# Two attention layers with mixture-of-experts and integer feed-forward: order of queues and small additions around the TensorE stream

## The chip, the cores and the metric

The kernel runs on one core of a Trainium2 chip, as one program. The metric is the device time in microseconds (us), of which a median of several runs is given. The engines are named as in the profile: PE is TensorE, PEld its weight loads, DVE is VectorE, ACT is ScalarE, POOL is GpSimd, SP is SyncE, which issues most of the transfers.

## What is computed

Eight sequences (B = 8) of 512 tokens with 512 features, in fp32, go through two post-norm layers:

```python
x = layernorm(x + L0_attn(x, ...))   # 16 heads of 32, causal softmax, biases on Q, K, V and the output
x = layernorm(x + L0_ffn(x, ...))    # 8 experts, top 2 of a softmax; LoRA on gate, gate/up and down
x = layernorm(x + L1_attn(x, ...))   # RMS-scaled input, 8 heads of 64, 2 key/value heads, no mask
x = layernorm(x + L1_ffn(x, ...))    # (wq - 128) * scale for gate, up, down; 1408 hidden, silu(gate) * up
```

In layer 0's attention, `scores = where(causal, -inf, q k^T / sqrt(32))`, then softmax and a product with v. In the experts, each token's two routing weights are divided by their sum, and the LoRA terms (`2 * B A`) may be added to the weights beforehand.

## The kernel before

**Layer 0's attention** (`attention0`, L1296) goes batch by batch, about 85 us each. A batch has four head groups g of four heads, and a group three units u of its keys (UNITS: key tile 0; tiles 1 and 3; tile 2). For each unit PE computes scores `sc` (`scores`, L1461), ACT takes their exponential into `p` (L1476), POOL clears the upper triangle of the diagonal blocks by an `affine_select` for each key tile of the unit (L1486), and later PE multiplies `p` by the values into `av` (L1503, `product`). DVE adds the units' `p` to a total (L1511), PE sums it into `rs` (L1518), and `normalise` (L1514) takes the inverse and scales `av` into `aoT` (L1522). `guard.watch_inverses` (L1076) adds the inverses to a running sum `g_total` on POOL; it is part of a check whether the fast path may be kept. The bias of the output projection is added to the residual `x` on POOL, all four tiles of a batch in one 128x2048 operation at group 2 (L1595).

Beside a batch's units, a list `todo[g, u]` (`plan`, L1527) puts other work of earlier batches: the output projection and layernorm of the batch before, its turn to features by rows (x1T), router logits (`score`, L1433), `choose` (top two, ranks), `dispatch`, and `one_hot` with `enter` (L1458, `Router.enter` L596), which writes a table of tokens through the PSUM bank `ps_table`. For most batches the turn goes through DRAM (class `Turn`, L83): DVE transposes 32x32 blocks, `out` (L100) writes them in four transfers (turned<-x1T), and `back` (L105) returns them as x1T in one transfer of 1 MB. LoRA terms of the experts are made beside u = 2's scores (`Experts.pair`, L805): ACT scales them, and for half of the weights a `load` brings the weights (merged<-in_gate_up), POOL adds the scaled term (L823) and a store writes them (L824); `merging` holds these for later units: load at unit n + i, add at n + 1 + i, store at n + 2 + i, for i = 0, 1. Next inputs are loaded by `load_xT` at g == 2 and `load_x` at g == 3, 1 MB each.

PE's order within a batch is written out; the order on DVE, ACT, POOL and SP in this stage is set when the kernel is built, by a scheduler with estimated times. The last batch's rest and the first tiles of the experts are interleaved at the end of `attention0`, with all engines in the written order: `tiles.step()` (L1013) does one tile of 128 tokens of one expert (gate and up `half`, turn of the hidden rows, `down`).

**The experts' stage** goes on with such steps. Rows of results are written to DRAM and gathered.

**Layer 1's attention** (`Attention1.run`, L1758) has DVE, ACT, POOL and PE in written order. A batch gathers two expert rows a token (`fetch`), adds them (`add`), sums them with the residual, turns the rows through DRAM (`Turn`), and computes its units. In `usual_pass` (L1953) the residual rows of batches 2 to 7 are loaded by SP at the start of this stage, twelve transfers of 512 KB, and after them the first integer weights and `w_out`.

**The integer FFN** (`IntegerFfn.run`, L1191) computes gate and up (ps_g, ps_u, L1222) and the output (ps_f, L1238), with x and h split in a high and a low part. Its first batch starts behind the last batch's residual and norm in layer 1 (`norm`, L1819, x L1804). Its last tile is normalised by `last_rows` (L1278): statistics on DVE, rstd on POOL, one `tensor_scalar` (L1288), and a store by ACT.

Of the kernel before, what the change touches and what calls it, by code (L numbers as in the profile page):

```python
# [19 lines left out]
NB = 8  # L20
# [62 lines left out]
class Turn:  # L83
# [21 lines left out]
    def back(self, room):  # L105
        self.nc.sync.dma_start(out=room, in_=self.dram.rearrange("p k i f -> p (k i f)"))
# [320 lines left out]
class Router:  # L427
# [4 lines left out]
    def __init__(self, env, keep, pool, small, tmp, dram):  # L432
# [39 lines left out]
        lane = pool.tile([P, 1], F32, name="r_lane")  # L472
# [4 lines left out]
        i = tmp.tile([P, S], F32, tag="r_inv", name="r_columns_i", bufs=2)[:, : E * E_TILES].bitcast(I32)  # L477
# [118 lines left out]
    def enter(self, ps, b, token, column, held, columns):  # L596
# [5 lines left out]
        nc.vector.tensor_tensor(self.table, ps, self.table, ALU.add)  # L602
        nc.vector.tensor_tensor(self.table, held, self.table, ALU.add)

# [4 lines left out]
    def soon(self, pool, ps, held):  # L609


        nc, half = self.nc, E // 2
        nc.tensor.matmul(ps, lhsT=self.ones, rhs=self.carry, start=True, stop=True)
        nc.vector.tensor_reduce(held, ps[:, :half], AX.X, ALU.min)
        nc.vector.tensor_scalar(held, held, float(SOON * P), None, ALU.is_ge)
        tokens = pool.tile([P, half, SOON], I32, name="t_soon")
        nc.vector.tensor_copy(tokens, self.by_expert()[:, :half, :SOON])
        return lambda e, j: tokens[:, e, j : j + 1]
# [10 lines left out]
    def tables(self, pool, ps, held):  # L629
# [9 lines left out]
        nc.vector.memset(tokens, 0)  # L639
        nc.tensor.matmul(ps, lhsT=self.ones, rhs=self.carry, start=True, stop=True)  # L640
        n_i = pool.tile([P, E], I32, name="t_n_i")
# [185 lines left out]
class Tiles:  # L827
# [185 lines left out]
    def step(self):  # L1013
# [10 lines left out]
        while self.fetched <= i + 10 and (self.fetched < self.n_soon or self.of_fixed is not None):  # L1024
            self.fetch(self.fetched)
            self.fetched += 1
        if i:
            self.down(i)
# [70 lines left out]
class IntegerWeights:  # L1099
# [16 lines left out]
    def load(self, pool, n, last):  # L1116
        start, end, unit = next(r for r in self.ranges if self.at < r[1] or r is self.ranges[-1])
        n = min(n, last - self.at, end - self.at)
        if n > 0:
# [3 lines left out]
            self.env.nc.sync.dma_start(out=slot, in_=src.rearrange("u p f -> p u f"))  # L1123
            self.slots.append((slot, self.at, n))
            self.at += n

# [18 lines left out]
class IntegerFfn:  # L1145
# [45 lines left out]
    def run(self, held_out, last_norm):  # L1191
        tc, nc, weights = self.env.tc, self.nc, self.weights
        with ExitStack() as phase:
            self.work = phase.enter_context(tc.tile_pool(name="d_work", bufs=1))
            self.p_gu = phase.enter_context(tc.tile_pool(name="d_gu", bufs=2, space=PSUM, reuse_waits="tile"))
            self.p_o = phase.enter_context(tc.tile_pool(name="d_o", bufs=1, space=PSUM, reuse_waits="tile"))
# [81 lines left out]
    def last_rows(self, b, t, x):  # L1278
# [8 lines left out]
        if t == NT - 1:  # L1287
            nc.vector.tensor_scalar(x, x, mv[:, 0:1], rstd, ALU.subtract, ALU.mult)  # L1288
# [4 lines left out]
        nc.scalar.dma_start(out=env.ins.out[b][ts(t, P), :], in_=x)  # L1293


def attention0(env, guard, keep, routes, experts, dram, p_mm, tiles_ctx):  # L1296
# [8 lines left out]
    with ExitStack() as phase:  # L1305
# [103 lines left out]
        turns = Turn(env, dram, NT, "turned0")  # L1409

# [3 lines left out]
        def blocks(b):  # L1414
# [5 lines left out]
            turns.back(flat)  # L1420
# [37 lines left out]
        def enter(rows, mm=mm, columns=HD):  # L1458
            router.enter(mm([P, E * E_TILES], "ps_table"), *rows, columns)

        def scores(b, g, u):  # L1461
# [22 lines left out]
            for kt in UNITS[u]:  # L1484
                first = p[:, :, at : at + P]
                nc.gpsimd.affine_select(out=first, in_=first, pattern=[[0, 4], [1, P]], compare_op=ALU.is_ge, fill=0.0,  # L1486
                                        base=0, channel_multiplier=-1)
                at += S - P * kt
            for thunk in merging.pop(n, []):
                thunk()  # L1490
# [23 lines left out]
        def normalise(b, g, acc):  # L1514
# [7 lines left out]
            nc.vector.tensor_tensor(aoTs[b][:, g, :], av, r_inv, ALU.mult)  # L1522
            guard.watch_inverses(r_inv)

        merging = {}

        def plan(b):  # L1527
# [26 lines left out]
            if b > 1:  # L1554
                todo[0, 0].append(lambda: choose(b - 2, mm=aside))
                todo[1, 0].append(lambda: dispatch(b - 2))
                todo[1, 2].append(lambda: enter(one_hot(b - 2, range(NT))))
# [21 lines left out]
        def soon():  # L1579
            tiles.of_soon = router.soon(routes, mm([P, E], "ps_count"), guard.routed[:, 0:1])  # L1580
# [7 lines left out]
        for b in range(NB):  # L1588
            todo, late = plan(b)
            for g in range(ND):  # L1590
                if g == 2:
                    if b + 1 < NB:
                        load_xT(b + 1)

                    nc.gpsimd.tensor_tensor(xs[b], xs[b], row[:, 1:2, :].to_broadcast([P, NT, D]), ALU.add)  # L1595
                if g == 3 and b + 1 < NB:
                    load_x(b + 1)
# [44 lines left out]
        choose(b, P)  # L1642
# [662 lines left out]
```

## Time and profile before

| | |
|---|---|
| median of 3 runs | 2105.66 us (2105.58 to 2105.78) |
| the profiled execution | 2106.08 us |
| its span | 2104.2 us |
| granted TensorE clock | 0.999 |
| PE busy | 2074.4 us |
| first matmul starts, last ends | 4.6 and 2095.25 us after the span's start |
| transfers issued by SP and ACT (queues q1, q10) | 175.34 and 1.07 MB |
| transfers issued by POOL (q0) | 34.61 MB |

Times of single events are counted from the span's start. Layer 0's attention takes the time to about 683 us, the experts to 1064, layer 1's attention to 1607 and the FFN to the end. "x <- y" in a line of waits means: an instruction of the first engine and line stood until the second was done; the numbers are us in all, times, and the longest.

### The profile page before, as it was taken

The numbers are of one execution on the slowest core, as the hardware profiler recorded it, in microseconds if no ns is written. First come the engines' busy times: TensorE is split into PE (matmuls) and PEld (weight loads), VectorE is DVE, ScalarE is ACT, GpSimd is POOL, SyncE is SP. The second block draws the span as 40 slices with busy tenths as digits, with TensorE's granted clock in tenths as the row PEclk, the third lists the DMA queues.
The fourth block names the chain that finished last, engine by engine and source line by source line (L and its number), as shares of the span: only waits on it lengthen the run. The fifth ranks groups of instructions, "written<-read, shape, count | busy, mean of one in ns | idle before, by whom it ended". The sixth has DMA issues, their size and how long they took to land. (4 is left out here: it accounts for less than half of the span.)

```text
span 2104.2 us, 35813 instructions
## 1 busy us (share of the span) xinstructions
PE 2074.4 (99%) x15074; PEld 1048.8 (50%) x15074; DVE 1270.6 (60%) x1963; ACT 606.8 (29%) x840; POOL 496.0 (24%) x488
## 2 busy tenths in 40 slices
PE   8999999999999999999999999999999999999998
PEld 2333333333334677774433333333335888888886
DVE  2666776776768623234257898887867644555443
ACT  2333433324333111111143333333332322222222
POOL 2343534434333221222042221223101000000000
PEclk9999999999999999999999999999999999999999
DMA  9020303415222568877451322132102311111000
GB/s 326 22 65 38 101 22 110 136 52 156 85 98 102 172 199 239 251 227 209 149 206 51 100 81 71 56 95 81 41 1 71 100 41 61 60 61 60 21 21 22
DMA packets 181946, 213.39 MB, mean 101 GB/s; under 512 B 72570, under 2 KB 125818, under 8 KB 178706
## 3 DMA queue, kind: packets, MB, share of 16 engines
q1 hardware_dynamic: 170496, 175.34, 26.8%
q0 software_dynamic: 10560, 34.61, 5.6%
q8 instruction: 121, 1.98, 0.4%
q10 hardware_dynamic: 722, 1.07, 0.1%
q14 instruction: 47, 0.39, 0.1%
HBM read 132.58 MB, written 78.40 MB: 100 GB/s over the span
## 5 line engine op out<-in xcount | busy, mean ns | idle before, releaser
L1077 POOL TENSOR_TENSOR g_total<-g_total,r_inv 128x512 f32<-128x512 f32 x64 | 90.1, 1408 | 488.3 <-DVE r_inv L1862 269.9
L1476 ACT ACTIVATE p<-sc 128x2048 f32<-128x2048 f32 (+1 forms) x96 | 153.0, 1594 | 174.7 <-PE sc L65 150.7
L1511 DVE TENSOR_TENSOR p<-p 128x1536 f32<-128x1536 f32 (+2 forms) x96 | 149.5, 1557 | 77.6 <-POOL p L1486 74.4
L1227 DVE SCALAR_TENSOR_TENSOR hT<-ps_u,vec,sg 128x512 f32<-128x512 f32 x88 | 65.6, 745 | 187.2 <-PE ps_u L1222 187.1
L1238 PE MATMUL ps_f<-ffn_w,h_half 128*128 128x512 f32 x664 | 168.1, 393 | 2.6 <-DVE h_half L1233 2.0
L958 PE MATMUL ps_gu<-xrT,experts 128*128 128x256 f32 x736 | 166.7, 380 | 0.4 <-DMA xrT<-pair 0.4
L958 PEld LDWEIGHTS ps_gu<-xrT,experts 128*128 128x128 f32 x736 | 139.5, 190 | 35.6 <-issue 19.2
L1832 ACT ACTIVATE p<-sc 128x1024 f32<-128x1024 f32 x128 | 124.2, 1022 | 100.2 <-PE sc L65 91.5
L1862 DVE RECIPROCAL r_inv<-r_inv 128x512 f32<-128x512 f32 x32 | 107.1, 3346 | 67.8 <-ACT r_inv L1074 67.8
L1238 PEld LDWEIGHTS ps_f<-ffn_w,h_half 128*128 128x128 f32 x664 | 122.9, 188 | 34.6 <-DVE h_half L1233 8.0
L1222 PE MATMUL ps_g<-x_high,ffn_w 128*128 128x512 f32 x352 | 137.3, 390 | 0.9 <-DVE x L1804 0.9
L1222 PE MATMUL ps_g<-x_low,ffn_w 128*128 128x512 f32 x352 | 137.2, 390 | 0.0
L1222 PE MATMUL ps_u<-x_low,ffn_w 128*128 128x512 f32 x352 | 137.1, 390 | 0.0
L1222 PE MATMUL ps_u<-x_high,ffn_w 128*128 128x512 f32 x352 | 137.1, 389 | 0.0
L65 PE MATMUL sc<-qT,kT 64*64 64x512 f32 x1024 | 124.7, 602 | 1.2 <-ACT qT L1729 0.9
L65 PE MATMUL ps_q<-experts 128*32 128x512 f32 x1024 | 120.8, 601 | 4.9 <-DMA experts<-in_xT 4.6
L65 PE MATMUL ps_v<-experts 128*32 128x512 f32 x1024 | 120.9, 595 | 0.0
L1851 PE MATMUL av<-p,v 128*64 128x512 f32 x512 | 120.9, 594 | 0.0
L1486 POOL TENSOR_SCALAR_AFFINE_SELECT p<-p 128x512 f32<-128x512 f32 x128 | 82.7, 657 | 157.6 <-ACT p L1476 155.0
L1225 ACT ACTIVATE sg<-ps_g,vec 128x512 f32<-128x512 f32 x88 | 60.6, 689 | 199.8 <-PE ps_g L1222 199.8
L65 PE MATMUL ps_o<-attn_out,aoT 128*64 128x512 f32 x512 | 116.4, 598 | 0.0
L65 PE MATMUL ps_k<-experts 128*32 128x512 f32 x1024 | 116.3, 595 | 0.0
(278 smaller groups left out, 3248.3 us busy)
## 6 DMA issues: line engine op xcount, KB each, us to landing
results<-y SPq DMA_DIRECT2D x68, 256.0 KB, 3.2
pair<-xrT SPq DMA_DIRECT2D x30, 512.0 KB, 3.0
xrT<-pair SPq DMA_DIRECT2D x120, 128.0 KB, 3.8
turned<-turned SPq DMA_DIRECT2D x56, 256.0 KB, 4.0
x<-in_x SPq DMA_DIRECT2D x8, 1024.0 KB, 8.6
rows<-x SPq DMA_DIRECT2D x32, 256.0 KB, 2.3
x<-rows SPq DMA_DIRECT2D x16, 512.0 KB, 12.5
experts<-in_xT SPq DMA_DIRECT2D x7, 1024.0 KB, 8.5
```

The costliest lines, as they stand in the source:

```text
L65: nc.tensor.matmul(out[m], lhsT=lhsT[:, m], rhs=rhs, start=start, stop=stop)
L958: nc.tensor.matmul(ps[:, j, :], lhsT=w, rhs=xT[:, c, :], start=c == 0, stop=c == ND - 1)
L1077: self.nc.gpsimd.tensor_tensor(self.total, self.total, r_inv, ALU.add)
L1222: nc.tensor.matmul(ps, lhsT=w[:, ts(dc, P)], rhs=x[:, dc, :], start=(dc, i) == (0, 0), stop=(dc, i) == (ND - 1, 1))
L1227: nc.vector.scalar_tensor_tensor(hT, u, vec[:, V_SU + c : V_SU + c + 1], sg, ALU.mult, ALU.mult)
L1238: self.nc.tensor.matmul(os[t], lhsT=h[:, ts(t, P)], rhs=self.weights(2 * NHID + c), start=(c, i) == (0, 0), stop=(c, i) == (NHID - 1, 1))
L1476: nc.scalar.activation(p, sc[:, :, :width], AF.Exp, scale=scale)
L1486: nc.gpsimd.affine_select(out=first, in_=first, pattern=[[0, 4], [1, P]], compare_op=ALU.is_ge, fill=0.0, base=0, channel_multiplier=-1)
L1511: nc.vector.tensor_tensor(total[:, :, P * kt :], total[:, :, P * kt :], p[:, :, at : at + w], ALU.add)
L1832: nc.scalar.activation(p, sc, AF.Exp, scale=scale)
L1851: nc.tensor.matmul(st["av"][HD * j : HD * (j + 1), :], lhsT=st["v"][:, kt, HD * j : HD * (j + 1)], rhs=p[:, j, :], start=kt == 0, stop=kt ...
L1862: nc.vector.reciprocal(r_inv, r_inv)
```

## The change

The edits, in the order of the diff:

- `Turn.back` hands out its instruction. In layer 0's attention `behind_return` makes `load_xT` (now at g == 0 from the second batch on), `load_x` and the merging transfers issue behind the last return in SP's queue.
- POOL's bias add goes tile by tile, 128x512 behind the selects of each group's unit 1 (the first batch keeps one add); the sum of inverses goes behind the select of the next unit 2.
- The table's bank is read ahead of the last normalisation in the last batch (`behind`). The count of `soon` is made in `tables`, from a kept copy of `carry`; `choose` of the last batch goes into the middle of a step (`amid`).
- Layer 1: the rows of batches 3 to 7 are loaded behind a batch's return by SP; the rows of batch 2, `w_out` and the first integer weights are issued by ScalarE in the first batch. The first batch's add of tile 0 of the next batch comes one step later.
- FFN: the pool of ps_o is opened before that of ps_g and ps_u, and two of layer 1's output banks use the other half of their tile; this maps the tiles to other banks. The last tile is normalised and stored in two halves, by SP and ScalarE.
- A constant of lane numbers shares a temporary tile (left out below).

```diff
     def back(self, room):
-        self.nc.sync.dma_start(out=room, in_=self.dram.rearrange("p k i f -> p (k i f)"))
+        return self.nc.sync.dma_start(out=room, in_=self.dram.rearrange("p k i f -> p (k i f)"))
...
-        nc.vector.tensor_tensor(self.table, ps, self.table, ALU.add)
+        read = nc.vector.tensor_tensor(self.table, ps, self.table, ALU.add)
...
+        return read
...
-    def soon(self, pool, ps, held):
+    def soon(self, pool):
...
-        nc.tensor.matmul(ps, lhsT=self.ones, rhs=self.carry, start=True, stop=True)
-        nc.vector.tensor_reduce(held, ps[:, :half], AX.X, ALU.min)
-        nc.vector.tensor_scalar(held, held, float(SOON * P), None, ALU.is_ge)
+        self.soon_carry = pool.tile([P, half], F32, name="r_soon_carry")
+        nc.vector.tensor_copy(self.soon_carry, self.carry[:, :half])
...
-    def tables(self, pool, ps, held):
+    def tables(self, pool, ps, held_soon, held):
...
+        half = E // 2
+        ps, soon = ps[:, :E], ps[:, E:]
...
+        nc.tensor.matmul(soon, lhsT=self.ones, rhs=self.soon_carry, start=True, stop=True)
+        nc.vector.tensor_reduce(held_soon, soon, AX.X, ALU.min)
+        nc.vector.tensor_scalar(held_soon, held_soon, float(SOON * P), None, ALU.is_ge)
...
             self.turn_rows(i, self.nc.scalar.copy)
...
-    def step(self):
+    def step(self, amid=lambda: None):
...
             self.fetched += 1
+        amid()
         if i:
             self.down(i)
...
 
-    def load(self, pool, n, last):
+    def load(self, pool, n, last, queue=None):
...
-            self.env.nc.sync.dma_start(out=slot, in_=src.rearrange("u p f -> p u f"))
...
+            if queue is not None:
+                return lambda: queue.dma_start(out=slot, in_=src.rearrange("u p f -> p u f"))
+            self.env.nc.sync.dma_start(out=slot, in_=src.rearrange("u p f -> p u f"))
...
+            self.p_o = phase.enter_context(tc.tile_pool(name="d_o", bufs=1, space=PSUM, reuse_waits="tile"))
...
-            self.p_o = phase.enter_context(tc.tile_pool(name="d_o", bufs=1, space=PSUM, reuse_waits="tile"))
...
         if t == NT - 1:
-            nc.vector.tensor_scalar(x, x, mv[:, 0:1], rstd, ALU.subtract, ALU.mult)
+            for i, queue in enumerate((nc.sync, nc.scalar)):
+                half = x[:, ts(i, D // 2)]
+                nc.vector.tensor_scalar(half, half, mv[:, 0:1], rstd, ALU.subtract, ALU.mult)
+                queue.dma_start(out=env.ins.out[b][ts(t, P), ts(i, D // 2)], in_=half)
...
-        nc.scalar.dma_start(out=env.ins.out[b][ts(t, P), :], in_=x)
+            nc.scalar.dma_start(out=env.ins.out[b][ts(t, P), :], in_=x)
...
         turns = Turn(env, dram, NT, "turned0")
+        returned = [None]
+
+        def behind_return():
+            return tc.issue_after(returned[0].ins) if returned[0] else ExitStack()
...
             turns.out(flat)
-            turns.back(flat)
+            returned[0] = turns.back(flat)
...
         def enter(rows, mm=mm, columns=HD):
-            router.enter(mm([P, E * E_TILES], "ps_table"), *rows, columns)
+            return router.enter(mm([P, E * E_TILES], "ps_table"), *rows, columns)
...
                 first = p[:, :, at : at + P]
-                nc.gpsimd.affine_select(out=first, in_=first, pattern=[[0, 4], [1, P]], compare_op=ALU.is_ge, fill=0.0,
-                                        base=0, channel_multiplier=-1)
+                select = nc.gpsimd.affine_select(out=first, in_=first, pattern=[[0, 4], [1, P]], compare_op=ALU.is_ge,
+                                                 fill=0.0, base=0, channel_multiplier=-1)
                 at += S - P * kt
-            for thunk in merging.pop(n, []):
-                thunk()
+            if u == 2 and inverses:
+                with tc.issue_after(select.ins):
+                    guard.watch_inverses(inverses.pop())
+            if u == 1 and b:
+                with tc.issue_after(select.ins):
+                    for t in ((0, 1), (2,), (3,), ())[g] if b == NB - 1 else (g,):
+                        x = xs[b][:, t, :]
+                        nc.gpsimd.tensor_tensor(x, x, row[:, 1, :], ALU.add)
+            elif (g, u) == (2, 1):
+                with tc.issue_after(select.ins):
+                    nc.gpsimd.tensor_tensor(xs[b], xs[b], row[:, 1:2, :].to_broadcast([P, NT, D]), ALU.add)
+            with behind_return():
+                for thunk in merging.pop(n, []):
+                    thunk()
...
             nc.vector.reciprocal(r_inv, r_inv)
-            nc.vector.tensor_tensor(aoTs[b][:, g, :], av, r_inv, ALU.mult)
-            guard.watch_inverses(r_inv)
-
-        merging = {}
+            normed[0] = nc.vector.tensor_tensor(aoTs[b][:, g, :], av, r_inv, ALU.mult)
+            if (b, g) == (NB - 1, ND - 1):
+                guard.watch_inverses(r_inv)
+            else:
+                inverses.append(r_inv)
+
+        merging, inverses, normed = {}, [], [None]
+
+        def behind(first, second):
+            tc.add_manual_dep(second.ins, first.ins.name,
+                              mybir.DependencyInfo(mybir.DependencyClass.NoSync, mybir.DependencyReason.DATA),
+                              reason="reads of a bank that is wanted")
...
-                todo[1, 2].append(lambda: enter(one_hot(b - 2, range(NT))))
+                if last:
+                    todo[1, 2].append(lambda: behind(enter(one_hot(b - 2, range(NT))), normed[0]))
+                else:
+                    todo[1, 2].append(lambda: enter(one_hot(b - 2, range(NT))))
...
         def soon():
-            tiles.of_soon = router.soon(routes, mm([P, E], "ps_count"), guard.routed[:, 0:1])
+            tiles.of_soon = router.soon(routes)
...
             for g in range(ND):
-                if g == 2:
-                    if b + 1 < NB:
+                if g == (0 if b else 2) and b + 1 < NB:
+                    with behind_return():
                         load_xT(b + 1)
-
-                    nc.gpsimd.tensor_tensor(xs[b], xs[b], row[:, 1:2, :].to_broadcast([P, NT, D]), ALU.add)
                 if g == 3 and b + 1 < NB:
-                    load_x(b + 1)
+                    with behind_return():
+                        load_x(b + 1)
...
         score(b)
-        choose(b, P)
+        tiles.step(lambda: choose(b, P))
...
-    return router, tiles, router.tables(routes, p_mm.tile([P, E], F32, tag="mm", name="ps_count"), guard.routed[:, 1:2])
+    return router, tiles, router.tables(routes, p_mm.tile([P, E + E // 2], F32, tag="mm", name="ps_count"), *(guard.routed[:, i : i + 1] for i in range(2)))
...
                 st["hT"] = own.tile([P, ND, S], F32, tag="hT", name="hT1")
-                self.turn.back(st["hT"].rearrange("p k s -> p (k s)"))
+                back = self.turn.back(st["hT"].rearrange("p k s -> p (k s)"))
+                if 2 <= b < NB - 1:
+                    with self.env.tc.issue_after(back.ins):
+                        self.load_rows(b + 1)
...
         state[0]["aoT"] = work.tile([P, ND, S], F32, tag="aoT", name="aoT1", bufs=2)
-        weights.load(work, 2, weights.FIRST)
+        load_first = weights.load(work, 2, weights.FIRST, nc.scalar)
...
-        for j in range(2):
-            nc.sync.dma_start(out=w_out[HD * j : HD * (j + 1), :, :],
-                              in_=env.ins.w_attn1[6 + 2 * j : 8 + 2 * j].rearrange("u (h p) f -> p (u h) f", p=HD))
+
+        def load_out():
+            for j in range(2):
+                nc.scalar.dma_start(out=w_out[HD * j : HD * (j + 1), :, :],
+                                    in_=env.ins.w_attn1[6 + 2 * j : 8 + 2 * j].rearrange("u (h p) f -> p (u h) f", p=HD))
+
...
                 todo[0] += [lambda t=t: pieces[1]["fetch"](t) for t in range(NT)]
+                todo[2] += [lambda: self.load_rows(2, nc.scalar), load_out]
+                todo[3].append(load_first)
...
                         todo[i + 2].append(lambda t=t: then["stat"](t))
-                for t, i in ((0, 1), (1, 2)) if first else ((0, 0), (1, 1), (2, 1), (3, 2)):
+                for t, i in ((0, 2), (1, 2)) if first else ((0, 0), (1, 1), (2, 1), (3, 2)):
...
         prepare_table(AF.Silu)
-        banks += [p_sc.tile([P, 2, S], F32, tag="sc", name="ps_o1")[:, 0, :] for _ in range(2)]
+        banks += [p_sc.tile([P, 2, S], F32, tag="sc", name="ps_o1")[:, 1, :] for _ in range(2)]
...
-                def load_rows(b):
+                def load_rows(b, queue=nc.sync):
...
-                        nc.sync.dma_start(out=env.xs[b][:, t : t + GAP // P, :], in_=rows.rearrange("(t p) d -> p t d", p=P))
+                        queue.dma_start(out=env.xs[b][:, t : t + GAP // P, :], in_=rows.rearrange("(t p) d -> p t d", p=P))
...
-            for b in range(2, NB):
-                load_rows(b)
+            attention.load_rows = load_rows
```

More of the change, by code (lines that the diff above doesn't have):

```diff
@@ L471, in __init__ @@
         nc.gpsimd.iota(i, pattern=[[0, 1]], base=0, channel_multiplier=1)
-        lane = pool.tile([P, 1], F32, name="r_lane")
+        room = tmp.tile([P, S], F32, tag="r_inv", name="r_columns_i", bufs=2)
+        lane = room[:, E * E_TILES : E * E_TILES + 1]
         nc.vector.tensor_copy(lane, i)
@@ L476, in __init__ @@
             nc.vector.tensor_scalar(self.signed[:, t : t + 1], lane, float(P * t - GAP + (P * t >= GAP)), None, ALU.add)
-        i = tmp.tile([P, S], F32, tag="r_inv", name="r_columns_i", bufs=2)[:, : E * E_TILES].bitcast(I32)
+        i = room[:, : E * E_TILES].bitcast(I32)
         nc.gpsimd.iota(i, pattern=[[1, E * E_TILES]], base=0, channel_multiplier=0)
```

## The prediction

> **What bounds the kernel now.** I read the page's busy times first.
>
> ```profile
> span 2104.2 us, 35813 instructions
> PE 2074.4 (99%) x15074; PEld 1048.8 (50%) x15074; DVE 1270.6 (60%) x1963; ACT 606.8 (29%) x840; POOL 496.0 (24%) x488
> ```
>
> TensorE (PE) is busy for 2074.4 of 2104.2 us at a granted clock of 0.999, and the change leaves its matmuls as they are: by the built orders of both kernels, one 128x8 count moves and a few groups swap places. So all that can be won is PE's idle time, 29.8 us: 4.6 before the first matmul, 9.0 after the last (2095.25 to 2104.25), 16.2 between. The chain of waits agrees: after PE no engine has over 4%.
>
> ```profile
> PE 42%; DVE 4%; POOL 1%; issue 1%; DMA 0%; ACT 0%; POOLq 0%; DVEq 0%; ACTq 0%
> ```
>
> Then PE's waits by what ended them (us in all, times, longest):
>
> ```profile
> PE ps_q L65 <- DMA experts<-in_xT: 4.6, 1, 4.6
> PE ps_f L1238 <- DVE h_half L1233: 2.0, 7, 0.5
> PE av L1503 <- POOL p L1486: 1.9, 3, 1.0
> PE ps_logits L504 <- DMA x1T<-turned: 1.8, 2, 1.5
> PE ps_x1T L1427 <- DVE g_routed L614: 1.5, 1, 1.5
> PE sc L65 <- ACT p L1476: 1.2, 1, 1.2
> ...
> PE ps_g L1222 <- DVE x L1804: 0.9, 1, 0.9
> ...
> PE ps_r L65 <- ACT logits L1440: 0.8, 1, 0.8
> PE ps_rank L65 <- DVE earlier L553: 0.7, 1, 0.7
> PE ps_f L1238 <- issue: 0.6, 1, 0.6
> ...
> PE rs L1859 <- DVE total L1840: 0.2, 1, 0.2
> ```
>
> About nine of these us belong to waits that the diff aims at. The timeline gives each a further cost: two matmuls in a row overlap, and a wait breaks that. A wait of 0.62 moved the next start by 0.78, one of 0.22 by 0.38; I add 0.165 to each.
>
> **Returns.** PE waits for the turned rows at 162.6 (0.30) and 417.5 (1.46): with the overlap 0.46 + 1.62 = 2.1. At 417.5 the timeline shows the cause: the writes of turned rows are issued at 400.1 to 403.9, the 1 MB load of x at 404.07, then the return at 408.74, which lands at 417.39, 8.6 us later. In the FFN stage a return with nothing ahead of it took 5.1 us (1935.77 to 1940.84). In the new order of SP's queue it stands ahead of x, so it should land at about 413.8; PE wants it at 416.06. Taken: 2.1 (0 to 2.1).
>
> **POOL.** At 163.9, 503.4 and 588.9 PE waits for the selects of unit u = 1: 0.27, 0.60, 1.01, with the overlap 2.4. The row ahead of them is the bias add, one 128x2048 of 4.55 us (498.21 to 502.73 in the second case). Four 128x512 adds cost about the 1.41 of the g_total row each, 5.6 for 4.55 a batch, but each stands behind u = 1's selects, and POOL, 24% busy, hides it. The g_total add (1.5) goes behind u = 2's select. A unit of PE's work is about 7 us; POOL's fullest now holds a select, g_total and two merged adds: 0.63 + 1.5 + 1.3 + 2.3 = 5.7. Taken: 2.4 (1 to 2.4); uncovered, POOL's extra 1.1 us a batch would cost up to 6 in six batches.
>
> **What the new SP order gives back.** Where the return is, one merged store and load now queue behind it, x's load follows, and then a load that waits for the store to land. In POOL's new order the merged add of the first load stands between u = 0's select and u = 1's two selects, in the three batches that merge through DRAM at that point (turned writes near 400, 486 and 571). Price: return 408.74 + 5.1 = 413.8; a store and a load of 256 KB behind it (two such stores landed 0.65 and 0.67 after a return at 586.08) bring the load to 415.2; the add takes 1.27 and the selects 1.23, so p is ready at 417.75, where av could start at 416.06 + 0.86 = 416.92. The wait is 0.8. The same sum gives 502.2 against 502.61 in the next batch and 587.65 against 587.67 in the third: nothing. Taken: -0.8 (0 to -3, if each landing is a microsecond late). The bias of x comes 20 us later, and xT is wanted a batch later: no cost.
>
> **Last batch and start of the experts.** The table bank was read late, so ps_x1T waits 1.46 at 649.1 and ps_q 0.35 after it. The read moves ahead of the last normalisation, but VectorE works without a pause from 634 to 653, and x1T still passes through it: I take 0.75 of the 1.8 + 0.33 (0 to 1.5). At 723.6 ps_r's wait of 0.76 + 0.165 goes, because a gate/up half is put before it; ps_rank, which waited 0.72 for VectorE 7 us later, now has VectorE's copy of y and two transposes (0.67 each) in its chain, and I add 0.5 to it. The wait of 0.44 + 0.165 for xrT at 758.4 probably goes, since a count and the tables stand ahead. Net +0.7 (-0.5 to 1.1). The select at 667 (1.19) and the wait at 670.7 (0.57) are not touched.
>
> **Layer 1's start.** Twelve loads, 6 MB, leave the front of SP's queue; the rest of rows and w_out is issued by ScalarE. The gathers of expert rows landed 7.9 us after issue in that crowd and about 4 later: with the first add moved one step, rs<-total (0.24 + 0.165) and two waits of 0.125 go: 0.6 (0.4 to 0.9). Before shows no such issues on ScalarE; SP's issues of the same tiles take 0.38 to 0.67, so four of them, 2.2 us, lie between two exps (end 1080.7 and start 1082.3). If that delay went through to rs at 1093.5 it would cost 1.6. Here the Trainium skill speaks against the change: "DMA: Bandwidth & Descriptors", section "Issuing engines are not separate DMA queues", says that loads from another issuer use the same 16 engines and save only issue time. By that rule ScalarE's queue gains nothing here, and may lose 1.6; by the rows the gain comes from 5 MB being asked for later, which it doesn't forbid. I keep 0.6 (-1.6 to 0.9).
>
> **FFN's start.** ps_g waits for x (0.85 + 0.165) behind VectorE's two parts; the new order of banks lets ps_f's halves interleave. hT's low half then waits for the x that POOL's rstd holds and a 1.22 conversion: ready at 1616.1, wanted at 1614.65, so a wait of 1.45 takes the place of 0.62 + 0.165 and of the split 0.33. Net 0.5 (0 to 1).
>
> **Last store.** The last 128x512 is normalised in 0.55 and its store takes 2.5 (2099.40 to 2101.91). In two halves on two queues, half a normalisation, about 0.25, and some transfer would be saved, less a second fixed cost. [...]by its rule on issuers the halves share the engines and it is nil. I take 0.2 (-0.1 to 0.5).
>
> **Sum.** 2.1 + 2.4 - 0.8 + 0.75 + 0.7 + 0.6 + 0.5 + 0.2 = 6.45. From the profiled execution (2106.08; 1.9 of it around the span of 2104.2) that is 2099.63; the median of the runs is 0.42 below it, so 2099.2.
>
> **Rivals.** (1) All targeted waits go and nothing returns: the upper ends, 2.1 + 2.4 + 1.5 + 1.1 + 0.9 + 1.0 + 0.5 = 9.5, give 2096.2. For it: 4 us of PE's work stand behind most waits. Against it: VectorE's unbroken stretch at 634 to 653. Chance 0.13.
>
> (2) The waits change their names: VectorE bounds 649, ps_rank and ps_f's low half as well as before, only the returns and half of the selects are won, less 0.8: 2.1 + 1.2 - 0.8 = 2.5, 2103.2. The case that the return, in the queue's real order, lands no earlier gives 2101.3. For it: VectorE is 60% busy, and turned writes end the same way whatever stands behind them. Chance 0.22.
>
> (3) Slower: the merged load. If the first load behind the return waits for a store to land, as the loads of before did (issued at 418.07, when the stores of 409.11 and 410.74 had landed), it is issued at 414.5 and lands 4.3 later (418.77 to 423.05 is the row), at 418.8. POOL stands at the add, here with its mean of 1.76, u = 1's selects end at 421.8, 4.1 after my 417.75, and in all three batches av waits that much longer, less the slack of 0.41 in the second: 11.9 us, 2111.1. In general a landing L later than I have it costs 3L - 0.4: the gain is gone from L = 2.3 on, and the kernel is slower by over 0.2% from L = 3.7 on. For it: POOL's order is fixed when the kernel is built, so the selects cannot pass the add. Against it: in the built order only the second load waits for the store behind the return, and its add stands behind the selects. Chance 0.10, with other losses of this size (ScalarE's issues).
>
> The forecast has 0.55, with its own 2097.3 to 2101.3. Chances: a change of 0.2%, 4.2 us, is about what this kernel's measurement can tell from none, so faster is below 2101.4: 0.55 + 0.13 and a few hundredths of (2), 0.70; within: 0.20; slower 0.10. The range leaves out what of (1) goes beyond its sum, the far end of (2), and (3): 2096.2 to 2105.0.
>
> **What would show it.** In the changed profile: ps_logits<-turned gone or under 0.3 in all; the return issued as long after its turned writes as before and landing about 5 us on; av<-POOL p left with one wait of about 0.8 at 417; ps_rank's wait over 1 us and ps_r's gone; ps_f's wait at 1616 about 1.4 and ps_g's gone; rs<-total gone. Wrong if POOL's merged add waits for a DMA over 2 us beyond its turn, if new waits appear near 1080 to 1095, or if PE's busy time leaves 2074.4 by over a microsecond.

## The result and the profile after

The changed kernel takes 2119.26 us (median of 6 runs, 2115.28 to 2125.32) where the kernel before takes 2105.62 (6 runs, 2103.37 to 2106.39): a ratio of 1.007, 95% interval 1.0053 to 1.0087. It is slower by about 13.6 us. I had forecast 2099.2. The profiled execution took 2116.91 us with a span of 2115.1 and a granted clock of 0.996; the sums below are made against its span.

The page's busy times and the chain, of the changed kernel:

```profile
span 2115.1 us, 35868 instructions
...
PE 2077.7 (98%) x15074; PEld 1048.2 (50%) x15074; DVE 1276.5 (60%) x1965; ACT 607.7 (29%) x840; POOL 507.2 (24%) x509
...
PE 46%; DVE 2%; POOL 0%; issue 0%; ACT 0%; DMA 0%; DVEq 0%; ACTq 0%
```

PE has the same 15074 matmuls, but is busy 3.3 us longer, and idle 37.4 us instead of 29.8. Its waits (us in all, times, longest):

```profile
PE sc L65 <- ACT scaled L817: 9.8, 3, 3.3
PE ps_q L65 <- DMA experts<-in_xT: 4.4, 1, 4.4
PE av L1531 <- POOL p L1502: 4.0, 3, 1.7
...
PE ps_f L1247 <- PE ps_u L1231: 0.8, 1, 0.8
PE ps_x1T L1443 <- DVE r_table L603: 0.7, 1, 0.7
PE ps_rank L65 <- DVE earlier L554: 0.7, 1, 0.7
```

The lines that the change aimed at are gone or shorter: no ps_logits<-turned, no ps_r, no xrT, no ps_g, no rs<-total, and ps_x1T waits 0.7 where it waited 1.5. The first line is new: before, PE never waited for `scaled`. And the waits of av on POOL's selects, which were to go, have doubled.

Marks in the two traces (start of the same matmul group, from the span's start) show where the time came from:

| mark | before | after | after less before |
|---|---|---|---|
| values of the fifth batch | 333.5 | 332.5 | -1.0 |
| of the sixth | 419.2 | 417.6 | -1.6 |
| of the seventh | 504.3 | 507.1 | +2.8 |
| of the eighth | 589.8 | 598.1 | +8.3 |
| output projection at 619 | 618.8 | 633.3 | +14.5 |
| the next one, behind the table | 688.9 | 702.6 | +13.7 |
| first values of layer 1 | 1051.9 | 1064.3 | +12.4 |
| of its next batch | 1184.7 | 1196.2 | +11.5 |
| the FFN's first ps_g | 1608.0 | 1618.8 | +10.8 |
| PE's last matmul ends | 2095.25 | 2105.63 | +10.4 |
| the span's end | 2104.2 | 2115.1 | +10.9 |

Three batches lose 16.1 us between them (from -1.6 to +14.5), and everything else wins, the tail excepted (+0.5). These are the batches in which weights are merged through DRAM beside a turn. The timeline of the changed kernel in the first of them (start, duration, engine and line, operation; in brackets the idle time before it and what ended it):

```profile
407.99 0.33 SPq L106 DMA_DIRECT2D x1T<-turned  x1
408.41 0.39 SPq L830 DMA_DIRECT2D merged<-merged  x1
...
408.85 0.46 SPq L827 DMA_DIRECT2D merged<-in_gate_up  x1
...
409.36 0.89 SPq L1342 DMA_DIRECT2D x<-in_x  x1
...
414.05 0.37 SPq L827 DMA_DIRECT2D merged<-in_gate_up  x1
...
414.78 1.27 POOL L829 TENSOR_TENSOR merged<-merged,scaled 128x512 f32<-128x512 f32 x1 [6.62 <-DMA merged<-in_gate_up]
...
416.01 1.22 POOL L1502 TENSOR_SCALAR_AFFINE_SELECT p<-p 128x512 f32<-128x512 f32 x2
...
416.70 1.07 PE L1531 MATMUL av<-p,v 128*32 128x384 f32 x16 [0.67 <-POOL p L1502]
417.20 2.76 POOL L1512 TENSOR_TENSOR x<-x,row 128x512 f32<-128x512 f32 x1
...
419.92 1.26 POOL L829 TENSOR_TENSOR merged<-merged,scaled 128x512 f32<-128x512 f32 x1
...
421.21 0.60 ACT L817 ACTIVATE scaled<-sc 128x512 f32<-128x512 f32 x1 [4.53 <-POOL merged L829]
...
421.86 1.12 PE L65 MATMUL sc<-q,k 32*64 32x512 f32 x16 [3.26 <-ACT scaled L817]
```

Read from the last line back. PE's next scores stand for 3.26 us, until ScalarE has read the bank; ScalarE's scaling stood for 4.53, because its one buffer `scaled` still held the last term, which POOL added only at 419.92 to 421.18; that add came behind u = 1's selects and the bias, and its load was issued at 414.05, when the store of 408.41 had landed, which stood behind the 1 MB return. (This trace has no landings; between 400 and 430 us SP waits 3.8 us for one such store, and in the run with two buffers below the store lands at 415.11 and the load goes at 415.13.) Upstream, POOL had already stood 6.62 us at the first merged add, with the selects behind it, and av waited 0.67 for them. The return itself was in time: ps_logits did not wait.

The clock is the second part. The same kernel in stretches of 2 to 4 us around the last of these waits (us, PE, PEld, DVE, ACT, POOL busy, granted clock, DMA share, GB/s):

```profile
598.00:602.00 4.00, 1.16 (x14) 0.25 (x6) 4.00 (x2) 0.23 (x1) 4.00 (x3) 0.93 0.30 76
602.00:604.00 2.00, 1.58 (x16) 0.33 (x16) 2.00 (x4) 0.84 (x2) 1.51 (x2) 0.50 0.61 214
604.00:606.00 2.00, 2.00 (x16) 0.40 (x12) 1.41 (x1) 1.47 (x1) 2.00 (x2) 0.50 0.43 121
606.00:608.00 2.00, 2.00 (x16) 0.59 (x12) 0.00 (x0) 0.41 (x1) 1.78 (x3) 0.50 0.28 100
608.00:610.00 2.00, 2.00 (x21) 0.48 (x16) 0.03 (x1) 0.00 (x0) 0.61 (x2) 0.94 0.48 172
```

PE waited 1.54 and 3.26 us around 597 and 602, and then its clock is at half for 6.8 us. Two such drops, 1.7 us of full clock lost behind the second batch's waits and 3.4 at the third's, make the difference between 0.999 and 0.996. The kernel before shows none at its waits of up to 1.46.

The 16.1 us are then: three waits of sc, 3 x (3.26 + 0.165) = 10.3; av's waits in the last two batches, 1.74 + 1.54 against 0.60 + 1.01, 1.7 more; and 4.1 left, against 5.1 us of clock lost, 0.5 of which fell into the last wait (half clock from 601.43 on, PE stood until 602.42).

### The profile page after: what moved, and what is told of

Its sections match the earlier page's. It is cut to its first block, busy times and chain, and to the rows that moved or that the text cites. A ratio compares the mean times of both kernels' runs of the same rounds, so it can differ in the third digit from the quotient of the medians.

```text
span 2115.1 us, 35868 instructions
## 1 busy us (share of the span) xinstructions
PE 2077.7 (98%) x15074; PEld 1048.2 (50%) x15074; DVE 1276.5 (60%) x1965; ACT 607.7 (29%) x840; POOL 507.2 (24%) x509
## 5 line engine op out<-in xcount | busy, mean ns | idle before, releaser
L1539 DVE TENSOR_TENSOR p<-p 128x1536 f32<-128x1536 f32 (+2 forms) x96 | 137.5, 1432 | 44.9 <-POOL p L1502 27.0
L1502 POOL TENSOR_SCALAR_AFFINE_SELECT p<-p 128x512 f32<-128x512 f32 x128 | 87.1, 692 | 288.0 <-ACT p L1492 264.8
```

The lines of the kernel that those rows point to most:

```text
L1502: select = nc.gpsimd.affine_select(out=first, in_=first, pattern=[[0, 4], [1, P]], compare_op=ALU.is_ge, fill=0.0, base=0, channel_multipl ...
L1539: nc.vector.tensor_tensor(total[:, :, P * kt :], total[:, :, P * kt :], p[:, :, at : at + w], ALU.add)
```

## The experiments

Theory A: the merged transfers, once behind the return, make POOL's second merged add late, and this reaches PE through ScalarE's single `scaled` buffer and the PSUM bank; the first add, ahead of the selects, is a smaller second path. Rival B: POOL's order (the first add ahead of the selects) is what costs. Rival C: another edit, or the clock alone. Every run was timed beside the kernel before on the same chip, whose median was 2105.73 for the first four, 2107.07 for the next four and 2107.04 for the last two.

**The merging transfers free of the return.**

```diff
-            with behind_return():
-                for thunk in merging.pop(n, []):
-                    thunk()
+            for thunk in merging.pop(n, []):
+                thunk()
```

> The changed kernel with the merging transfers no longer held behind the return (the loads of x and xT still are). In its built order both merged loads of a pair are issued ahead of the turned writes, as in the kernel before. Theory A (the merged transfers behind the return make POOL's second merged add late; ScalarE's next scaling waits for that add, and PE's scores for the PSUM bank that the scaling reads): the three waits of sc on scaled and of av on POOL's selects in the middle batches go, the granted clock is 0.999 again, and the time is about 2098 us (2096 to 2101). Rival B (what hurts is POOL's order, which puts the first merged add ahead of unit 1's selects): the same here, as that order goes too. Rival C (another edit, or the clock by itself, makes the kernel slower): it stays above 2110.

Measured: 2103.41 us, ratio 0.999 (0.9984 to 0.9997). PE's waits in its trace:

```profile
PE ps_logits L505 <- DMA x1T<-turned: 2.5, 2, 1.5
PE ps_f L1247 <- DVE h_half L1242: 2.0, 7, 0.5
PE ps_logits L505 <- ACT scaled L817: 1.7, 1, 1.7
```

The waits of sc and of av are gone, so C falls; A and B are not told apart. But it is 5 us above what I expected: the return is late again. In SP's queue the stores of merged weights now stand ahead of it and wait for POOL's adds (408.94 and 410.18), and the return leaves at 410.77 although the turned writes had landed at 407.7. One of its waits, of 1.73 us, was followed by half clock for 3.4 us.

**The merging transfers behind the return, as the only edit to the kernel before.**

```diff
-            for thunk in merging.pop(n, []):
-                thunk()
+            with behind_return():
+                for thunk in merging.pop(n, []):
+                    thunk()
```

> The kernel before with one edit of the change alone: the merging transfers behind the return. In its built order x is still loaded ahead of the return. Theory A: in three batches PE waits for scaled and for POOL's selects, 4 to 7 us each, and the clock falls for some us behind these waits: 2117 to 2128 us. Rival C: it stays within 2 us of before, 2104 to 2108.

Measured: 2120.41 us, ratio 1.0073 (1.0057 to 1.0088), clock 0.997:

```profile
PE av L1508 <- POOL p L1490: 8.9, 6, 3.9
PE ps_q L65 <- DMA experts<-in_xT: 4.6, 1, 4.6
PE sc L65 <- ACT scaled L811: 2.8, 2, 2.0
```

This one edit is enough to make the whole loss. In this order more of it arrives by av and less by sc; the cause is common, the path is not.

**The router's logits four times in the three batches**, so that PE works where it stood (only the last pass counts).

```diff
-            router.logits(x1Ts.pop(b), ps)
+            x1T = x1Ts.pop(b)
+            for _ in range(4 if b in (3, 4, 5) else 1):
+                router.logits(x1T, ps)
```

> The changed kernel with the router's logits of three batches computed four times over in place of once: 24 more matmuls, 3.2 us of PE's work, ahead of the waits of each of the three middle batches; the last pass gives the values. If the waits end at a time that PE does not set (POOL and transfers), the added work lies inside them: av's wait and most of sc's go, and the time is not longer in spite of 9.5 us more work. If in addition the clock was lost because PE stood still, it stays at 0.999, and the time falls to about 2112 us (2109 to 2115), with less spread than the 2115 to 2125 of the changed kernel. If the clock is lost for another reason, or the waits were PE's own, it is 2119 to 2128.

Measured: 2116.27 us (2114.8 to 2117.66), ratio 1.0053 (1.0039 to 1.0067), clock 0.998. That is a microsecond above my range. The added work is 7.7 us, not 9.5: in the trace ps_logits takes 3.64 in place of 1.07, 2.57 more a batch. It cost nothing, so the waits' end is not PE's. av's waits are gone; those of sc (3.41, 2.69, 3.79) are not shorter, for two reasons in the trace: in the first batch the return left 1.46 later (409.45) and the second add ended about as much later (422.7), and two ps_v matmuls (1.0 us), which the changed kernel has ahead of these scores, come behind them here. Of the clock, one stretch of 3.4 us at half is left instead of three. The changed kernel, run once more beside later kernels, took 2117.74 (2115.13 to 2122.31), so that the time proves nothing of the clock; the count of half stretches in the two traces is all there is.

**The first merged add behind u = 1's selects and bias.**

```diff
+        def add():
+            with self.env.tc.issue_after(self.select.ins):
+                nc.gpsimd.tensor_tensor(w[0], w[0], scaled, ALU.add)
...
+        if i == 0:
+            return {0: load, 2: lambda: (add(), store())}
+        return {1: load, 2: add, 3: store}
...
+            experts.select = select
```

> The changed kernel with the first merged add moved behind unit 1's selects and the bias, so that these no longer wait for the merged load; the transfers stay behind the return. Theory A (the second add, whose load follows a store's landing, sets when PE goes on): av's waits go, sc's waits on scaled grow by as much, and the time is 2114 to 2121 us, not to be told from the changed kernel. Rival B (POOL's order is the cause): both waits go or shrink by over half, 2100 to 2108 us.

Measured: 2128.53 us, ratio 1.0108 (1.0093 to 1.0124). av's waits are gone and sc's have grown from 9.8 to 14.3:

```profile
PE sc L65 <- ACT scaled L817: 14.3, 3, 5.2
...
PE rs L1555 <- DVE q L1404: 4.6, 3, 1.5
PE rs L1555 <- DVE v L1393: 2.5, 3, 1.6
```

The second add in the first of the three batches:

```profile
424.47 1.26 POOL L831 TENSOR_TENSOR merged<-merged,scaled 128x512 f32<-128x512 f32 x1 [3.37 <-DMA merged<-in_gate_up]
```

That is A: PE goes on when the second add is done, and a wait taken away ahead of it comes back there. POOL now has nothing to do ahead of that add and stands 3.37 us for its load; yet the add ends 12.96 us behind the issue of the return (412.77), in the changed kernel 13.19 (407.99 to 421.18). So neither the selects nor the bias add make it late, and B falls. The time is 7 us above A's range, and that is my edit's doing. It moves the adds in every group that merges, also beside small operations of VectorE, and rs waits 7.1 us for VectorE there, which does not wait for the selects but is slow. Ahead of the first of these six waits:

```profile
373.32 2.51 POOL L831 TENSOR_TENSOR merged<-merged,scaled 128x512 f32<-128x512 f32 x2
373.33 1.35 DVE L593 TENSOR_SCALAR one_hot<-r_columns,r_to_column 128x256 bf16<-128x256 bf16 x1
...
375.80 0.27 DVE L593 TENSOR_SCALAR one_hot<-r_columns,r_to_column 128x256 bf16<-128x256 bf16 x1
```

The same operation takes 1.35 us beside POOL's adds and 0.27 behind them; at the other five it is alike. The clock adds to it: 17.1 us at half in this trace, 10.2 in the changed kernel's.

**Two buffers for the second half's scaled term** (rounded to bf16 for room, which changes the merged weights a little).

```diff
-        scaled = own.tile([P, 2, 256], F32, tag=f"scaled{i}", name="scaled")
+        scaled = own.tile([P, 2, 256], BF16 if i else F32, tag=f"scaled{i}", name="scaled", bufs=1 + i)
```

> The changed kernel with two buffers for the second half's scaled LoRA term, so that ScalarE can scale the next term while POOL's add of the last one is late. To fit, this term is rounded to bf16, so the second half's merged weights differ a little. POOL's order and the transfers stay. Theory A (the long wait reaches PE through ScalarE's single buffer): the three waits of sc on scaled, 9.8 us, go; av's waits on POOL's selects stay, 0.7 to 1.8 us each; with less of the clock lost the time is 2103 to 2109. If PE would anyway be held at the same time by another consumer of POOL's late work, a wait of the same size appears beside it and the time stays at 2115 to 2121.

Measured: 2103.49 us, ratio 0.9983 (0.9975 to 0.9992), clock 0.999:

```profile
PE av L1531 <- POOL p L1502: 5.0, 3, 1.7
PE ps_q L65 <- DMA experts<-in_xT: 4.6, 1, 4.6
PE ps_f L1247 <- DVE h_half L1242: 2.0, 7, 0.5
```

The decisive one. Transfers and POOL's order are as in the changed kernel (in its first of these batches the second load is issued at 415.13, and the add ends at 422.34), and yet no wait for `scaled` is left, and about 14 us with it. The late second add costs only through ScalarE's buffer. The first path, av's 1.6 to 1.7 a batch, stays. With the waits the half clock is gone too; what of the 14 us is wait and what is clock, the times alone don't part.

**The changed kernel again**, beside these.

> The changed kernel as it is, beside the others on one chip, for the comparison of times and of the granted clock: 2115 to 2121 us, clock 0.995 to 0.997.

Measured: 2117.74 us, ratio 1.0053 (1.0039 to 1.0066); sc's waits are 9.8 again, and half clock is lost behind all three batches this time (1.7, 1.7 and 3.4 us of full clock).

**Only the merged stores behind the return.**

```diff
+        def store():
+            with self.behind():
+                nc.sync.dma_start(out=self.merged[:, e : e + 2, f], in_=w[0])
...
-                2 + i: lambda: nc.sync.dma_start(out=self.merged[:, e : e + 2, f], in_=w[0])}
+                2 + i: store}
...
-            with behind_return():
-                for thunk in merging.pop(n, []):
-                    thunk()
+            for thunk in merging.pop(n, []):
+                thunk()
...
+        experts.behind = behind_return
```

> The changed kernel with only the merged stores behind the return; the merged loads go as soon as their buffer is free, in the built order one of them well ahead of the turned writes. In the run with all merging transfers free, the stores waited in SP's queue for POOL ahead of the return, and the return left 3 us late (410.8 after turned writes that had landed at 407.7). Theory A: the return leaves within 0.5 us of the turned writes' landing, ps_logits waits under 0.5 us in all, no wait for scaled, and the time is 2097 to 2101. If the sum of the gains was too high (rest of the change worth less), it is 2101 to 2105.

Measured: 2119.79 us, ratio 1.0059 (1.0045 to 1.0073). I was wrong by 20 us, and the timeline says why:

```profile
408.95 0.33 SPq L106 DMA_DIRECT2D x1T<-turned  x1
...
409.37 0.39 SPq L831 DMA_DIRECT2D merged<-merged  x1
...
415.02 0.37 SPq L827 DMA_DIRECT2D merged<-in_gate_up  x1
...
420.05 1.26 POOL L833 TENSOR_TENSOR merged<-merged,scaled 128x512 f32<-128x512 f32 x1 [10.12 <-DMA merged<-in_gate_up]
...
421.95 1.94 PE L1536 MATMUL av<-p,v 128*32 128x384 f32 x16 [5.38 <-POOL p L1508]
```

One store, the second half's of the group before, still falls behind the return; the next load of that half needs its buffer and goes at 415.02, and now POOL's add of it stands ahead of u = 1's selects. The same late load reaches PE by av, 15.4 us in three waits.

**The same, with the last tile whole.**

```diff
-            for i, queue in enumerate((nc.sync, nc.scalar)):
-                half = x[:, ts(i, D // 2)]
...
+            nc.vector.tensor_scalar(x, x, mv[:, 0:1], rstd, ALU.subtract, ALU.mult)
```

> The kernel with only the merged stores behind the return, and the last tile normalised and stored whole by ScalarE as before. By my forecast the halves win 0.2 us, so this is 0.2 slower than its neighbour; by the traces (4.32 us from PE's last matmul to the end of the last normalisation with halves, 4.13 without; a half takes 0.41 of the whole's 0.55) it is 0.2 to 0.5 faster.

Measured: 2120.7 us (2117.74 to 2121.98) beside 2119.79 (2117.57 to 2121.39). This doesn't decide a few tenths. The traces are steadier: from PE's last matmul to the span's end 8.94 us whole and 9.13 in halves, here; over all traces 8.94 to 9.00 in the three with the whole tile, 9.09 to 9.50 in the nine with halves. So the halves lose 0.1 to 0.5.

**The second half's store a unit earlier, so that no store is caught behind the return; loads free.**

```diff
+        if i:
+            return {1: load, 2: lambda: (add(), store())}
+        return {0: load, 1: add, 2: store}
```

> As the kernel with only the merged stores behind the return, but the second half's store follows its add at once, a unit earlier, so that it is not behind the return: in its trace that store (409.4, landed 415.0) held the second half's next load (415.0, landed 419.9), and POOL's add of it stood ahead of unit 1's selects. In the built order both merged loads now come ahead of the turned writes and the next stores behind return and x. Theory A (a merged store behind the return makes the next load and add late, whatever stands behind that add): no wait for scaled or POOL's selects, ps_logits under 0.5 us in all, clock 0.999, and 2097 to 2101 us. If the returns win less than I think, or another wait takes their place, 2101 to 2105.

Measured: 2098.76 us (2097.96 to 2099.72), ratio 0.9961 (0.9947 to 0.9974), clock 0.999. It is faster than both kernels. In its trace

```profile
407.95 3.50 POOL L834 TENSOR_TENSOR merged<-merged,scaled 128x512 f32<-128x512 f32 x2
...
409.16 0.33 SPq L106 DMA_DIRECT2D x1T<-turned  x1
...
412.20 1.22 POOL L1512 TENSOR_SCALAR_AFFINE_SELECT p<-p 128x512 f32<-128x512 f32 x2 [0.16 <-ACT p L1502]
...
416.36 1.06 PE L505 MATMUL ps_logits<-x1T,r_wr 128*32 128x512 f32 x8
...
417.25 1.05 PE L1540 MATMUL av<-p,v 128*32 128x384 f32 x16
...
417.46 1.08 ACT L817 ACTIVATE scaled<-sc 128x512 f32<-128x512 f32 x2
```

both adds are done at 411.45, before the returned rows have landed (414.11), the selects are early, and PE has no wait of over 0.1 us between 16 and 645 us; from the third batch's values on, they follow each other by 84.25 us.

**The rest of the change alone:** the edits to queues and POOL in layer 0's batches undone.

> The changed kernel with its edits to queues and POOL in layer 0's batches undone (loads of x and xT, merging, bias and sums of inverses as before), and the rest kept: the table's read, the experts' start, layer 1's loads, the FFN's banks, the halves of the last store. The marks of the changed kernel's trace behind the middle batches say that the rest wins 0.8 at the table, 1.3 at the experts, 0.9 at layer 1, 1.0 at the FFN and loses 0.3 in the tail: 3.7 in all, about 2102 us (2101 to 2103). My forecast's terms for the same parts sum to 2.75: 2103. If they are only given back elsewhere: 2105 or more.

Measured: 2101.71 us, ratio 0.9979 (0.997 to 0.9988), 4.4 us by the ratio: the rest wins about what the marks said. The kernel with the early store, beside it on the same chip, is 3.0 faster still; that is what the edits to queues and POOL are worth when no merged transfer is late. Of its waits in the batches, av<-POOL (2.3 us in 4) and ps_logits (0.2) are what the queue edits were for.

## Why the prediction was wrong

**The failed step** is "What the new SP order gives back ... The wait is 0.8", and in it the sentence on the second merged load in rival (3): "its add stands behind the selects". I followed POOL's late work to one reader, the selects and av. In the first batch that term was right: av waited 0.67 + 0.165 for a forecast 0.8. (In the next two the first add began 8.4 and 7.0 us behind the issue of the return, 6.8 in the first, and av waited 1.74 and 1.54 where I had nothing.) But the second add has a reader of its own: ScalarE's buffer `scaled`, and behind it the bank that PE's scores need. Behind the selects did not mean harmless. The runs show the size of what I left out: 9.8 us of waits of sc, and with the clock about 14 us between the changed kernel (2117.74) and that with two buffers (2103.49). Two of my own signs of being wrong came true: POOL's first merged add stood 6.6 to 7.7 us for its load, and PE's busy time left 2074.4 by 3.3.

**Rival (3)** had the place and over half of the price (11.9 us above the forecast, of 20), but by the wrong path: the load that waited for a store was the second one, the first came as I had it, and av was not where most was lost. I gave it 0.10; its own question, who waits for the second add, was not asked.

**The clock** was in no term. It goes from 0.997 to 0.993 between the fastest run of the changed kernel (2115.28) and the slowest (2125.32), which is about 8 of these 10 us. The Trainium skill, "TensorE: Matmul & The Clock Gate", Part 1, says that an idle window of about 3.4 us takes the clock to half, and that the window runs freely. The traces agree on the depth (0.50), the unit (3.41 us) and the free run, but the window needn't be idle: the clock fell behind windows in which PE worked for up to 0.49 of the time (last section). So it was in part luck whether a wait of 3.3 us cost nothing, as in the first batch of the profiled run, or 1.7 or 3.4 us, as in the next two.

**The other terms.** Returns and selects, forecast 2.1 + 2.4, won 4.6 where nothing was given back: from the first batch's values to the eighth's (16.4 to 586.6), the kernel with the early store takes 570.2 us, before 574.8 (15.0 to 589.8). Beside the kernel with the rest alone (574.0) it is 3.8: there ps_logits waits only 0.2 in all, with SP's order in these batches as before, so the 1.6 that I had for the wait at 417.5 is not in every kernel with the old order. The table, 0.75: 0.8. The experts' start, 0.7: 1.3, because ps_rank's wait stayed 0.7, where I had feared another 0.5. Layer 1, 0.6: 0.9, although ps_hT now waits 0.7 at 1117, where three waits took 0.5; the bound of -1.6 for ScalarE's issues did not show, and the skill's rule on issuers was no bar, since the loads were moved in time. FFN, 0.5: 1.1, with ps_f's new wait only 0.78, not 1.45. The tail, +0.2: a loss of 0.5 in this trace; a half takes 0.41 and the whole 0.55, so the second half is ready later (4.32 us behind PE's last matmul, the whole at 4.13). These terms sum to 3.6 against a forecast 2.75, and the run with them alone is 0.21% faster than before. Two readings were off, without weight: VectorE did pause before 653 (1.80 us until 638.02, 0.77 until 651.87), and ScalarE's operation behind the exp that ends at 1080.7 starts at 1082.73.

So the sum, 0.31%, fits the kernel in which the merged transfers hold nobody (0.39% faster than before, 0.26 to 0.53), and that was not the kernel I had to forecast.

## What to carry to other kernels

When a transfer is moved behind another in a queue, follow the buffer that it fills or frees through every engine to PE, and not only to the nearest reader: here store, load, add, scaling buffer, PSUM bank, scores. A single buffer between two engines ties them together, and here a second one (or an earlier free) was worth 14 to 19 us, the place in the queue 3 to 5. And price a wait of PE of more than one or two microseconds with what the clock may lose by it, here up to 3.4 us.

## What the runs showed of the hardware

**The clock.** At PE's waits the granted clock fell to 0.50, for 3.41 or 6.83 us and nothing in between, which costs 1.7 or 3.4 us. Within a trace the starts of half clock lie whole multiples of 3.413 us apart (26 and 468 of them in the changed kernel's, 441 in that with four logits), so there is a grid of such stretches. Cut along it, the twelve traces show 19 starts between 20 and 2080 us, and each follows a stretch in which PE was busy for less than half (at most 0.49). Of the stretches at full clock, every one of 0.43 or less was followed by half clock (17), two of the six between 0.43 and 0.5, none above. (The ends of matmuls are modelled, so these shares are near values.) Where a wait falls on the grid decides: one of 3.25 us in the changed kernel, two thirds of it in one stretch, cost half clock; one of 3.41 in the kernel with four logits, spread over two about evenly, cost nothing. So did a wait of 1.73 cost 3.4 us at half clock in one run, in a stretch of 0.49, while three of 1.6 to 1.7 did not. The changed kernel first, then that with four logits:

```profile
509.27:512.69 3.42, 1.30 (x20) 0.39 (x24) 3.42 (x3) 1.16 (x3) 2.94 (x4) 1.00 0.72 266
512.69:516.10 3.41, 3.41 (x20) 0.87 (x16) 1.70 (x2) 1.79 (x1) 1.89 (x2) 0.50 0.50 147
...
418.39:421.80 3.41, 1.61 (x24) 0.52 (x16) 3.41 (x2) 0.00 (x0) 3.41 (x3) 1.00 0.74 240
421.80:425.22 3.42, 1.80 (x24) 0.52 (x28) 3.42 (x4) 1.66 (x3) 2.94 (x3) 1.00 0.90 321
```

**POOL beside VectorE.** POOL's 128x512 add took 2.76 us at 417.20 and 1.26 at 419.92. The second lies wholly beside VectorE's reciprocal (418.76 to 422.11), so that is not the reason. Before 640 us, 265 of POOL's 128x512 adds in the twelve traces took over 2 us. All of them lie beside a VectorE addition of `p` to the total, and all end 1.12 to 1.15 us after that addition, as if they began then; 162 with nothing of VectorE beside them took 1.16 to 1.29. The other way round it is the same: VectorE's operation of 0.27 us took 1.35 beside POOL's adds.

**SP's transfers** landed in the order of their issue. A 256 KB store and a load issued 0.4 and 0.9 us behind the 1 MB return of 408.97 landed at 415.1 and 416.0, and x, issued 0.5 later, at 418.7 (the run with two buffers). In the traces that have landings, 1127 pairs of neighbours in SP's queue between 20 and 690 us have both recorded, and none overtook the one before.
